# A four-layer graph kernel: the first attention stripe leaves out its last row group, which follows the start of the second stripe

## The chip, the cores and the metric

The kernel runs on one core of a Trainium2 chip. The metric is the device time of one execution in microseconds (us); the time before is the median of three runs. TensorE (PE) multiplies matrices into PSUM banks, ScalarE (ACT) applies functions and copies, VectorE (DVE) and GpSimd (POOL) work elementwise, SyncE (SP) issues most of the DMA transfers. Every engine takes its own instructions strictly in the order in which they were built, and waits at an instruction whose inputs are not there. What stands behind a waiting instruction on the same engine waits with it.

## The reference, cut to what matters

`x` has 4096 rows of 64 numbers, `adj` is a 4096 x 4096 matrix of zeros and ones. Four layers follow each other, each of the form `x = layernorm(x + layer(x, adj))`. Layers 1 and 3 are attention in hyperbolic space, and only they are touched by the change:

```
x_t   = logmap0(x)
left  = x_t @ w[:D];  right = x_t @ w[D:]
adj_att   = sigmoid(left[:, None] + right[None, :] + b) * adj
x_local   = logmap(x[:, None, :], x[None, :, :])
support_t = einsum('ij,ijd->id', adj_att, x_local)
out       = proj(expmap(x, support_t))
```

Layer 0 is a mean over neighbours with a matrix product and a normalisation, layer 2 a sum over neighbours with weights that halve from one neighbour to the next. Each layer reads the whole of `adj` again (268 MB in four passes).

## The kernel before, in words

**Tiles.** The output rows of a layer are cut into four *stripes* of 1024 (`GROUPS` = 3, 2, 1, 0, in this order), the source rows into 32 *blocks* of 128 (`BLOCKS`, from 31 down). Eight blocks are a *row group* with the same number as the stripe that holds the same rows. Two blocks are a *unit* `g` (15 down to 0): one transfer of 1 MB brings the edges of a unit (`load`, six buffers). A stripe of an attention layer thus has 16 units, four from each row group, and a layer 64 units. Units are counted here from 1 to 64 in the order of execution, in each attention layer.

**A unit** (`attend`, L1141 to L1216). For each of its two blocks: TensorE puts six matmuls into a PSUM tile `z` of 128 x 1024 (L1175, L1178, L1181; three `z` tiles exist); ScalarE makes `sig`, a sigmoid of `left` of the stripe and `right` of the block (L1136), and `sq`, a square of `z` (L1195); VectorE makes `t` = max(z, 0) * sig (L1198). Then VectorE combines the unit in one instruction of 128 x 2048 (L1203), and TensorE adds it, two units later, with float32 matmuls into `acc`, one PSUM bank (L1153; each counts as two passes in the profile). At the end of a stripe `acc` is copied by ScalarE to `sums` in SBUF (L1215). There is one `acc` bank, so the next stripe's first addition waits for that copy.

**Row work.** Whatever is done per row and not per pair is written as generators that give way at each `yield`; `tick` (after each block and unit, `rate` times) lets the queues of such generators go one step on, and the number that a generator yields is how many ticks it stays away. `later` puts a generator into one of three queues; a queue does its generators one after the other. `need(tag)` ticks until the named piece has been issued. The pieces:
- `end_0`, `norm_rows`, `prepare` (L1529 on, L929 on, L958 on): they end the layer before for one row group and make its inputs for the attention layer: `y`, the transposes `hi_lo`, `src`, `lo_hi`, `dst` (L1033 on TensorE, L1037 on ScalarE), `xe`, a logarithm (L1045, L1046 on ScalarE), `left` and `right`. For row group 0, the last one, most of this is on GpSimd ("pooled"): it is done while the first stripe of the attention layer already runs, since the first stripe needs row group 0 only in its last four units, 13 to 16.
- `far(small, large)` (L665) tells how many ticks such a chain on GpSimd takes: 0.29 us for a small and 1.04 us for a large operation, plus 3.9 us, divided by the length of a tick.
- `spread_left` (L1109): `left` of a stripe turned and copied to all partitions (L1117 on TensorE, two copies L1123 on ScalarE).
- `move(layer, s, sums, curve)`: after a stripe, its sums go through a centring product with the constant `centre` (L1286; L1265 for the very last stripe) to rows, and the map back to the next `x`. For stripes 3, 2, 1 the small operations are on GpSimd, with a few of them on VectorE (L1306, L1308, L783, L1353); for stripe 0 all are on VectorE.
- `supports` and `store`: what follows a moved stripe, for layer 2 or the output.

**Who orders.** In layers 0 and 2 the order on TensorE and ScalarE is that of the program. In the attention layers a scheduler in the compiler orders the instructions of every engine by its own estimate of when their inputs are there. From the second stripe on, `anchored` pins row work behind the pair work that was traced ahead of it; in the first stripe it may go where the scheduler likes.

`attention` (L1638) calls `attend` for stripes 3, 2, 1, 0. After each it queues the stripe's `move`. At the very end (L1825 on) a few VectorE operations fill `fits`, a test on the data; TensorE turns it (L1857), and only then does the last centring product (L1265) come on TensorE.

Of the kernel before, what the change touches and what calls it, by code (L numbers as in the profile page):

```python
# [19 lines left out]
P = 128  # L20
# [41 lines left out]
def gnn_stack_kernel(  # L62
# [504 lines left out]
    def stream(fits):  # L567

        with ExitStack() as st:
# [65 lines left out]
            def there(tag):  # L635
                while tag not in done:
                    yield 1
# [27 lines left out]
            def far(small, large=0):  # L665

                beat = {1: 0.8, 3: 0.4}.get(place[0], 1.6)
                return 1 + int((small * 0.29 + large * 1.04 + 3.9) / beat)

# [470 lines left out]

            def attend(layer, s, rate, then):  # L1141

                acc = ps.tile([P, W], F32, name="acc")
                if layer == 1 and s == GROUPS[0]:
                    spare.append(lambda dtype, shape: of_bank(acc, dtype, shape))
                lag, squares = [], []

                def add_up(g, t, ks, behind=None):

                    for k in ks:  # L1150
                        j = 2 * g + k
                        for h in range(2):
                            it = nc.tensor.matmul(  # L1153
                                acc[h * D : (h + 1) * D, :], xe[:, j, :],
                                t[:, k, h * W : (h + 1) * W],
                                start=j == BLOCKS[0], stop=j == BLOCKS[-1],
                            )
                            if behind is not None:
                                in_order(it.ins, behind.ins)

                for g in reversed(range(NB // 2)):
                    _, edge = load(s, g)
                    need((layer, 2 * g // WB))
                    if g == 4 and then is not None:
                        later(in_turn((layer, then, "left"), spread_left(then)), True)
                    for k in (1, 0):
# [17 lines left out]
                        if k == 1:  # L1184
                            if len(lag) == 2:
                                if spare:
                                    spare_ends()
                                add_up(*lag.pop(0), last)
                            sq = sb.tile([P, 2, WW], F32, name="sq")
                            t = sb.tile([P, 2, WW], F32, name="t", bufs=3)  # L1190
                            ts = [t, t]
                            if g == 0 and then is None and layer == 3:
                                ts[0] = sb.tile([P, 2, WW], F32, name="t", bufs=3)
# [18 lines left out]
                for args in lag:  # L1212
                    add_up(*args)
                sums = row.tile([P, W], F32, name="sums", bufs=2)
                nc.scalar.copy(sums, acc)  # L1215
                return sums  # L1216

            def to_rows_of(sums):

                t = take(F32, P, SB, 2, D)  # L1220
                for k in range(SB):
                    nc.tensor.transpose(t[:, k], sums[:, k * P : (k + 1) * P], ident)
                return t.rearrange("p k h f -> p h k f")

            def move(layer, s, sums, curve):
# [27 lines left out]
                if straight:  # L1253
# [5 lines left out]
                    for part in range(2):  # L1259
                        t = z_tile()[:, : 4 * (D + 1)].rearrange(  # L1260
                            "p (i h f) -> p i h f", i=2, h=2
                        )
                        for i in range(2):
                            cols = slice((2 * part + i) * P, (2 * part + i + 1) * P)
                            nc.tensor.matmul(  # L1265
                                t[:, i], sums[:, cols], centre, start=True, stop=True
                            )
                        parts.append(t)
# [12 lines left out]
                for part in () if straight else range(2):  # L1281
                    yield from free()
                    t = take(F32, P, 2, 2, D + 1)
                    for i in range(2):
                        cols = slice((2 * part + i) * P, (2 * part + i + 1) * P)
                        nc.tensor.matmul(t[:, i], sums[:, cols], centre, start=True, stop=True)  # L1286
                    yield near()
# [163 lines left out]
            with ExitStack() as lp:  # L1451
# [18 lines left out]

                x_ts = [row.tile([P, W], F32, name="sums", bufs=2)[: D + 1] for _ in range(2)]
                for x_t in x_ts:
# [89 lines left out]
                with tc.manual_schedule(engines=FIXED):  # L1562
                    for s in GROUPS:
# [44 lines left out]
                        if s == GROUPS[0]:  # L1608
                            need((0, s))
                            curve1, curve3, att1, att3 = made  # L1610
                        total = row.tile([P, W], F32, name="sums", bufs=2).rearrange(
                            "p (b d) -> p b d", d=D
# [25 lines left out]
            def attention(layer, curve, rates, behind):  # L1638

                need((layer, GROUPS[0]))  # L1640
                for n, s in enumerate(GROUPS):
                    if n:
                        need((layer, s, "turned"))
                        need((layer, s, "left"))
                    anchored[0] = n > 0
                    then = GROUPS[n + 1] if n + 1 < NW else None
                    if n == 0 and layer == 1:
                        later(end_0(GROUPS[-1], total, deg))
                    sums = attend(layer, s, rates[n], then)
                    move_s = in_turn((layer, s, "moved"), move(layer, s, sums, curve))  # L1650
                    if n:
                        later(
                            in_turn((layer + 1, s + 1), there((layer, s + 1, "moved")), behind(s + 1)),
                            True, 9,
                        )
                    apart = 2 if n + 1 == NW and layer == 1 else 0
                    later(move_s, apart)
                    if n + 1 == NW:
                        later(in_turn((layer + 1, s), behind(s)), apart)
                anchored[0] = False  # L1660
# [6 lines left out]
            )  # L1667
            attention(1, curve1, (2, 1, 1, 1), supports)

# [127 lines left out]
            with tc.manual_schedule(engines=FIXED):  # L1797
                spare.append(lambda dtype, shape: of_bank(row_bank, dtype, shape))

                for some in (GROUPS[:2], GROUPS[2:3], GROUPS[3:]):  # L1800
                    accs = wide_pass(some) if len(some) == 2 else narrow_pass(some[0])
                    for s, of in zip(some, accs):
                        sums = [row.tile([P, W], F32, name="sums", bufs=2) for _ in of]
                        for to, acc in zip(sums, of):
                            if s == GROUPS[-1]:
                                V.tensor_copy(to, acc)
                            else:
                                nc.scalar.copy(to, acc)
                        later(end_2(s, sums))
# [11 lines left out]
            with tc.issue_after(weighed[0].ins):  # L1821
                attention(3, curve3, (4, 1, 1, 1), store)

# [7 lines left out]

            sq = row.tile([P, D], F32, name="w_sq")
            V.memset(sq, 0.0)
            one = V.tensor_mul(sq[:D], w2_sb, w2_sb)
            in_order(one.ins, split[1].ins)
            ones = row.tile([P, 1], F32, name="w_ones")
            V.memset(ones, 1.0)
# [89 lines left out]
```

## Time and profile before

| | us |
|---|---|
| median of 3 runs (lowest, highest) | 1034.7 (1034.37, 1035.6) |
| the profiled execution's own time | 1035.3 |
| its span, first to last instruction | 1033.6 |
| PE / DVE / ACT / POOL busy | 940.1 / 910.2 / 747.0 / 333.9 |
| stretch of layer 0 | 0 to 171 |
| layer 1 (attention): its four stripes | 171, 260, 335, 412 to 488 |
| layer 2 | 488 to 692 |
| layer 3 (attention): its four stripes | 692, 779, 855, 931 to 1005 |
| last stripe's `move` and the output | 1005 to 1033.6 |

The execution has 1.7 us around its span, and is 0.6 us over the median of the runs. Mean granted TensorE clock 0.985. A row of the profile names line, engine, operation and tiles, then how often, busy us, mean ns of one, and the idle time of the engine just before it with what ended that idle time. In a timeline, a bracket at the end of a row is the engine's idle time before that row and the instruction that released it. "L1198 DVE" is line 1198 of the kernel, on VectorE; lines in the 760s and 780s are helpers that several callers share.

### The profile page before, as it was taken

The numbers are of one execution on the slowest core, as the hardware profiler recorded it, in microseconds if no ns is written. First come the engines' busy times: TensorE is split into PE (matmuls) and PEld (weight loads), VectorE is DVE, ScalarE is ACT, GpSimd is POOL, SyncE is SP. The second block draws the span as 40 slices with busy tenths as digits, with TensorE's granted clock in tenths as the row PEclk, the third lists the DMA queues.
The fourth block names the chain that finished last, engine by engine and source line by source line (L and its number), as shares of the span: only waits on it lengthen the run. The fifth ranks groups of instructions, "written<-read, shape, count | busy, mean of one in ns | idle before, by whom it ended". The sixth has DMA issues, their size and how long they took to land.

```text
span 1033.6 us, 14323 instructions
## 1 busy us (share of the span) xinstructions
PE 940.1 (91%) x5197; PEld 417.9 (40%) x5197; DVE 910.2 (88%) x1420; ACT 747.0 (72%) x866; POOL 333.9 (32%) x695
## 2 busy tenths in 40 slices
PE   7866767899999999999999999998999999999991
PEld 6755765233333333333333344442333333333320
DVE  7686797899999999999398499979999999999996
ACT  2102116789988988987677788888998898888860
POOL 0021211470255455365011020106302563662650
PEclk9999899999999999999999999999999999999996
DMA  9999999655666566575799998995465666665500
GB/s 369 425 427 425 397 426 425 260 189 204 235 216 230 200 224 224 179 244 204 268 351 351 373 335 311 337 325 198 164 244 201 213 240 216 239 209 208 205 10 14
DMA packets 38322, 271.68 MB, mean 263 GB/s; under 512 B 4255, under 2 KB 4577, under 8 KB 5474
## 3 DMA queue, kind: packets, MB, share of 16 engines
q1 hardware_dynamic: 37728, 270.03, 70.8%
q8 instruction: 42, 0.69, 0.3%
q10 hardware_dynamic: 514, 0.66, 0.2%
q14 instruction: 38, 0.31, 0.1%
HBM read 269.62 MB, written 1.05 MB: 262 GB/s over the span
## 4 chain that ended last, share of the span: by engine, by line
PE 60%; DVE 20%; DMA 7%; ACT 5%; POOL 5%; issue 2%; SPq 0%; ACTq 0%; POOLq 0%; DVEq 0%
PE acc L1153 17%; PE z L1774 11%; PE z L1175 8%; PE z L1181 7%; DVE t L1203 7%; PE z L1178 7%; DMA edges<-in_adj_dram 7%; DVE t L1198 6%; PE z L1786 3%; PE z L1740 2%; DVE junk L879 2%; ACT sq L1195 2%; PE acc L1584 2%; ACT sq L1781 1%; ACT sig L1136 1%
## 5 line engine op out<-in xcount | busy, mean ns | idle before, releaser
L1198 DVE SCALAR_TENSOR_TENSOR t<-z,sig 128x1024 f32<-128x1024 f32 x255 | 307.2, 1218 | 18.7 <-ACT sq L1195 16.5
L1195 ACT ACTIVATE sq<-z 128x1024 f32<-128x1024 f32 x256 | 255.2, 1023 | 60.0 <-PE z L1181 26.5
L1203 DVE SCALAR_TENSOR_TENSOR t<-sq,t 128x2048 f32<-128x2048 f32 x127 | 294.4, 2318 | 0.3
L1136 ACT ACTIVATE sig<-left_b,right 128x1024 f32<-128x1024 f32 x255 | 286.0, 1149 | 2.8 <-DVE t L1198 1.5
L1153 PE MATMUL acc<-t,xe 128*64 128x512 f32 x1024 | 256.6, 610 | 15.1 <-DVE t L1203 15.0
L1175 PE MATMUL z<-edges,two_i 128*128 128x512 bf16 x512 | 200.8, 392 | 2.5 <-DVE t L1198 1.5
L1181 PE MATMUL z<-dst,src 74*128 74x512 f16 x512 | 194.6, 380 | 0.0
L1178 PE MATMUL z<-lo_hi,hi_lo 128*128 128x512 f16 x512 | 193.6, 378 | 0.0
L1781 ACT ACTIVATE sq<-z 128x512 bf16<-128x512 f32 (+1 forms) x192 | 138.0, 740 | 39.8 <-PE z L1774 38.7
L1584 PE MATMUL acc<-parts,edges 128*128 128x193 bf16 x1024 | 100.2, 252 | 37.8 <-DMA edges<-in_adj_dram 37.0
L1153 PEld LDWEIGHTS acc<-t,xe 128*64 128x64 f32 x1024 | 64.0, 136 | 144.6 <-issue 105.6
L879 DVE SCALAR_TENSOR_TENSOR t<-edges 128x2048 bf16<-128x2048 f32 x41 | 94.0, 2308 | 20.0 <-DMA edges<-in_adj_dram 20.0
L1584 PEld LDWEIGHTS <-edges 128*128 128x128 bf16 x1024 | 86.7, 100 | 48.5 <-DMA edges<-in_adj_dram 46.4
L1175 PEld LDWEIGHTS <-two_i 128*128 128x128 bf16 x512 | 50.0, 98 | 121.7 <-issue 75.0
L1774 PE MATMUL z<-edges,pass_by 128*128 128x512 bf16 x248 | 86.5, 388 | 6.3 <-ACT sq L1781 5.7
L1774 PE MATMUL z<-edges,enter 128*128 128x512 bf16 x256 | 88.2, 387 | 0.0
L1181 PEld LDWEIGHTS <-src 74*128 74x128 f16 x512 | 49.1, 96 | 72.5 <-issue 10.3
L1178 PEld LDWEIGHTS <-hi_lo 128*128 128x128 f16 x512 | 50.2, 98 | 57.1 <-issue 11.5
L1303 POOL TENSOR_TENSOR w_att<-x,u 128x512 f32<-128x512 f32 x6 | 16.2, 2706 | 149.4 <-ACT u L1297 149.4
L979 ACT CAST ys<-y 128x512 f16<-128x512 f32 x8 | 4.9, 616 | 74.3 <-DVE y L976 44.6
L879 DVE SCALAR_TENSOR_TENSOR junk<-edges 128x2048 bf16<-128x2048 f32 x23 | 52.5, 2282 | 0.0
L1740 PE MATMUL z<-sq,halves 128*128 128x512 bf16 x128 | 48.0, 377 | 0.2 <-ACT sq L1781 0.2
(451 smaller groups left out, 906.4 us busy)
## 6 DMA issues: line engine op xcount, KB each, us to landing
edges<-in_adj_dram SPq DMA_DIRECT2D x256, 1024.0 KB, 5.0
x<-in_x_dram SPq DMA_DIRECT2D x2, 256.0 KB, 5.7
out_dram<-x ACTq DMA_DIRECT2D x2, 256.0 KB, 2.3
out_dram<-x SPq DMA_DIRECT2D x2, 256.0 KB, 2.8
x<-in_x_dram SPq DMA_DIRECT2D x1, 384.0 KB
x<-in_x_dram SPq DMA_DIRECT2D x1, 128.0 KB, 2.9
weights_sb<-in_weights_dram ACTq DMA_DIRECT2D x1, 96.0 KB, 5.5
enter_w<-in_enter_dram ACTq DMA_DIRECT2D x1, 32.5 KB
```

The source lines that it names most:

```text
L879: return V.scalar_tensor_tensor(junk, a, 0.0, a, ALU.not_equal, ALU.not_equal, accum_out=odd[:, n : n + 1])
L1136: one = nc.scalar.activation(sig, left_bs[s], AF.Sigmoid, bias=right[:, j : j + 1])
L1153: it = nc.tensor.matmul(acc[h * D : (h + 1) * D, :], xe[:, j, :], t[:, k, h * W : (h + 1) * W], start=j == BLOCKS[0], stop=j == BLOCKS[-1],)
L1175: nc.tensor.matmul(half, two_i, edge[:, at : at + W], start=True, stop=False)
L1178: nc.tensor.matmul(half, hi_lo[:, of], lo_hi[:, to], start=False, stop=False)
L1181: last = nc.tensor.matmul(half, src[:, of], dst[:, to], start=False, stop=True)
L1195: square = nc.scalar.activation(sq[:, k], zp, AF.Square, bias=ROOT + OFF, scale=-1.0 / UNIT)
L1198: V.scalar_tensor_tensor(ts[k][:, k], zp, 0.0, sig, ALU.max, ALU.mult)
L1203: V.scalar_tensor_tensor(t, sq, HIGH**2, t, ALU.add, ALU.mult)
L1584: nc.tensor.matmul(banks[i // 2][:, i % 2, :PARTS], edge[:, at : at + P], parts[:, j, :PARTS], start=j == BLOCKS[0] and i % 2 == 0, stop=j ...
L1774: nc.tensor.matmul(z[:, h : h + W], lhs, rhs[:, h : h + W], start=j == BLOCKS[0], stop=True, skip_group_check=True,)
L1781: weighed[0] = nc.scalar.activation(w, z[:, :n], AF.Exp, bias=-(OFF_EDGE + CUT) * LN2, scale=-LN2)
```

## The change

In each attention layer six *sections* take the place of four stripes:

| section | stripe | row groups | units in the order |
|---|---|---|---|
| 1 | 3 | 3, 2, 1 | 1 to 12 |
| 2 | 2 | 3 | 13 to 16 |
| 3 | 3 | 0 | 17 to 20 |
| 4 | 2 | 2, 1, 0 | 21 to 32 |
| 5 | 1 | all | 33 to 48 |
| 6 | 0 | all | 49 to 64 |

Sections 1 and 2 end with a copy of `acc` to a `sums` tile and nothing else. After sections 3 to 6 the stripe's `move` is queued; for stripes 3 and 2 it gets two `sums` tiles and adds them in the centring product, which becomes twice as many matmuls (`to_centre`). Row work is pinned from section 4 on. Stripe 2's `left` is spread from the third queue, five units ahead of the end of section 1. `far` counts 6.0 us instead of 3.9. A third `sums` buffer is added, and two small tiles of the last test are laid into a constant that is no longer used then.

```
-                return 1 + int((small * 0.29 + large * 1.04 + 3.9) / beat)
+                return 1 + int((small * 0.29 + large * 1.04 + 6.0) / beat)
...
-            def attend(layer, s, rate, then):
+            def attend(layer, s, rate, then, groups, final):
 
+                gs = [g for g in reversed(range(NB // 2)) if 2 * g // WB in groups]
+                j_first, j_last = 2 * gs[0] + 1, 2 * gs[-1]
                 acc = ps.tile([P, W], F32, name="acc")
...
-                                start=j == BLOCKS[0], stop=j == BLOCKS[-1],
+                                start=j == j_first, stop=j == j_last,
...
-                for g in reversed(range(NB // 2)):
+                for g in gs:
                     _, edge = load(s, g)
                     need((layer, 2 * g // WB))
-                    if g == 4 and then is not None:
-                        later(in_turn((layer, then, "left"), spread_left(then)), True)
+                    if g == gs[max(len(gs) - 5, 0)] and then is not None:
+                        later(
+                            in_turn((layer, then, "left"), spread_left(then)),
+                            2 if s == GROUPS[0] else 1,
+                        )
...
-                sums = row.tile([P, W], F32, name="sums", bufs=2)
+                sums = row.tile([P, W], F32, name="sums", bufs=3)
                 nc.scalar.copy(sums, acc)
                 return sums
...
+            def to_centre(to, sums, cols):
+
+                for n, part in enumerate(sums):
+                    nc.tensor.matmul(
+                        to, part[:, cols], centre, start=n == 0, stop=n + 1 == len(sums)
+                    )
...
-                        nc.tensor.matmul(t[:, i], sums[:, cols], centre, start=True, stop=True)
+                        to_centre(t[:, i], sums, cols)
...
-                for n, s in enumerate(GROUPS):
-                    if n:
+                g3, g2, g1, g0 = GROUPS
+                sections = (
+                    (g3, g2, (g3, g2, g1), False),
+                    (g2, None, (g3,), False),
+                    (g3, None, (g0,), True),
+                    (g2, g1, (g2, g1, g0), True),
+                    (g1, g0, GROUPS, True),
+                    (g0, None, GROUPS, True),
+                )
+                sums, before = {s: [] for s in GROUPS}, None
+                for n, (s, then, groups, final) in enumerate(sections):
+                    if n in (1, 4, 5):
                         need((layer, s, "turned"))
                         need((layer, s, "left"))
-                    anchored[0] = n > 0
-                    then = GROUPS[n + 1] if n + 1 < NW else None
+                    anchored[0] = n > 2
...
-                    sums = attend(layer, s, rates[n], then)
-                    move_s = in_turn((layer, s, "moved"), move(layer, s, sums, curve))
-                    if n:
+                    sums[s].append(attend(layer, s, rates[n], then, groups, final))
+                    if not final:
+                        continue
+                    move_s = in_turn((layer, s, "moved"), move(layer, s, sums[s], curve))
+                    if before is not None:
                         later(
...
-            attention(1, curve1, (2, 1, 1, 1), supports)
+            attention(1, curve1, (2, 2, 2, 1, 1, 1), supports)
...
-                attention(3, curve3, (4, 1, 1, 1), store)
+                attention(3, curve3, (4, 4, 4, 1, 1, 1), store)
...
-            sq = row.tile([P, D], F32, name="w_sq")
-            V.memset(sq, 0.0)
-            one = V.tensor_mul(sq[:D], w2_sb, w2_sb)
-            in_order(one.ins, split[1].ins)
-            ones = row.tile([P, 1], F32, name="w_ones")
+            sq, ones = enter_w[:D, :D], enter_w[:D, D : D + 1]
+            V.tensor_mul(sq, w2_sb, w2_sb)
             V.memset(ones, 1.0)
```

## The prediction

> **What bounds the kernel now.** I read the page first (VectorE 88% busy, TensorE 91%), then busy time by stretch, then VectorE's, ScalarE's and GpSimd's timelines in the first stripes, then the tail. First the stretches (each row: TensorE, its weight loads, VectorE, ScalarE, GpSimd busy, then clock and DMA share):
>
> ```profile
> 171.00:260.00 89.00, 81.18 (x378) 29.56 (x379) 80.24 (x88) 76.33 (x81) 34.15 (x56) 0.98 0.64 238
> 260.00:335.00 75.00, 75.00 (x334) 26.72 (x333) 74.04 (x55) 67.22 (x72) 35.18 (x88) 1.00 0.65 228
> 692.00:779.00 87.00, 80.68 (x392) 30.69 (x391) 81.12 (x87) 78.91 (x85) 24.61 (x43) 1.00 0.61 214
> 779.00:855.00 76.00, 76.00 (x333) 26.88 (x332) 73.69 (x54) 66.79 (x71) 37.34 (x88) 1.00 0.63 218
> ```
>
> Both attention layers behave alike. A later stripe takes 75 to 76 us with VectorE and TensorE full: the undisturbed unit is 4.57 us from one L1203 to the next (one combine, 2.20, and two L1198 at about 1.15). A first stripe takes 87 to 89. Of those 12 to 14 us, the row work of group 0 on VectorE is 8.7 in layer 1 and 7.4 in layer 3 (sum of its rows), which the change does not remove. The rest is VectorE idle: 7.1 in layer 1 from unit 2 on, 3.9 in layer 3. Who ends the idle time in layer 1:
>
> ```profile
> 189.44 0.69 DVE L932 TENSOR_REDUCE n_m<-z 128x8 f32<-128x512 f32 x1 [2.87 <-POOL z L1545]
> 210.72 0.20 DVE L970 RECIPROCAL rb<-b 128x8 f32<-128x8 f32 x1 [1.09 <-POOL b L967]
> 230.66 1.23 DVE L1198 SCALAR_TENSOR_TENSOR t<-z,sig 128x1024 f32<-128x1024 f32 x1 [0.72 <-ACT sq L1195]
> ```
>
> Two waits on GpSimd's chain, then small waits on ScalarE. The second kind has its cause on ScalarE's own timeline:
>
> ```profile
> 214.77 0.62 ACT L979 CAST ys<-y 128x512 f16<-128x512 f32 x1 [3.21 <-POOL y L976]
> 228.00 1.28 ACT L1045 ACT_TABLE_LOAD   x1
> 229.50 0.21 ACT L1045 ACTIVATE tt<-tt 128x8 f32<-128x8 f32 x1 [0.22 <-POOL tt L1015]
> 230.74 1.28 ACT L1136 ACT_TABLE_LOAD   x1
> 232.03 1.15 ACT L1136 ACTIVATE sig<-left_b,right 128x1024 f32<-128x1024 f32 x1
> ```
>
> ScalarE loses 3.21 on GpSimd, then has four copies L1037, the logarithms and two table loads to make up, beside 3.9 a unit of pair work. The logarithm met its input almost exactly (0.22). GpSimd's small operations take 0.20, but every eighth to tenth takes over 2:
>
> ```profile
> 226.51 2.35 POOL L798 TENSOR_TENSOR rt<-rs_t,rt 128x8 f32<-128x8 f32 x1
> 228.94 0.20 POOL L1014 TENSOR_TENSOR tt<-q,rt 128x8 f32<-128x8 f32 x1
> ```
>
> **The change part by part.** The idea has room for at most the idle time, 7.1 + 3.9 = 11 us. What of it goes is read from the built order of instructions of the changed kernel, with the durations above.
>
> *First stripe, layer 1.* Up to L932 VectorE's order is the same, so 2.87 stays. The second pair, L783 to L970, moves one unit later as a whole, with the same work between: 1.09 stays. Then the chain to the logarithm. Before, VectorE's L783 for it stands behind the 17th L1198, and L1045 behind ScalarE's 21st square: four blocks apart. After, L783 stands behind the 21st L1198 and L1045 behind the 22nd square: one apart, so that GpSimd has three blocks less, some 6 us. By hand: L984 at 224.3; GpSimd from L989 to the end of L1015 took 216.57 to 229.47, 12.9, with three long operations (12.9 - 3 x 2.15 = 6.4 without any); so its input comes between 230.8 and 237.3. ScalarE is there at 230.6. I take 2.3 long ones, 236: a wait of about 5. Behind it on ScalarE stand two squares, a table load and the next sigmoid (0.9 + 0.9 + 1.3 + 1.05); VectorE has two L1198 and a combine left, then stands until 240. Also the two logarithms are now apart with sigmoids between: four table loads for two, 2 x 1.29 = 2.6 more on ScalarE, which has 0.67 a unit to spare. Followed instruction by instruction, the 16th combine comes at 264 against 258.8 before. About 0.7 of that is made up where the copies L1123 went into ScalarE's idle 3.9 at 188. **+4.5 us, from 0 (no long operation) to +6.5.**
>
> [...]
>
> *First stripe, layer 3.* L783 to L970 has a combine less between (idle 1.37 becomes 3.6, +2.3). In exchange copies and row work, which before crowd into units 6 to 9 (1.87 idle in the ninth), spread over three more units. By hand the 12th combine (before at 757.9) comes at the same place within 0.1. **0, from -1.9 to +2.3.**
>
> *Two more section ends per layer, four in all.* Each drains two units into `acc` and copies it (0.59 on ScalarE, which has room). The unit after the first stripe's end lost 0.47 before. **4 x 0.3 = +1.2, from 0 to 2.0.**
>
> *Twice the centring matmuls for stripes 3 and 2.* Eight more passes a stripe. Four of them put the next matmul off by 0.45 (265.26 to 265.71) and 0.62, so 1.07 a stripe, 4.3 in all, on an engine with under 0.1 a unit to spare; VectorE's 1.34 of reductions beside it covers half. **+2.2, from 0 to 4.3.**
>
> *Stripes 2 and 1 move later.* Stripe 3's move starts four units later, and its queue is serial, so the moves of 2 and 1 start three to four units behind their stripe's end. Before, copies L1297 and L1304 met the section end and VectorE idled 0.99, 0.91, 0.99, 0.92 there (sum 3.8); apart from it I take half. **-1.9, from -3.8 to 0.**
>
> *The tail.* Stripe 1's move now isn't done when the last unit ends. Before:
>
> ```profile
> 1002.49 2.64 DVE L1203 SCALAR_TENSOR_TENSOR t<-sq,t 128x2048 f32<-128x2048 f32 x1
> 1005.05 1.21 DVE L1198 SCALAR_TENSOR_TENSOR t<-z,sig 128x1024 f32<-128x1024 f32 x1
> 1008.82 0.16 DVE L1843 TENSOR_TENSOR fits<-fits,g 128x1 f32<-128x1 f32 x1
> ...
> 1010.47 0.27 PE L1857 MATMUL fit_t<-ident,fits 128*1 128x128 f32 x1
> 1011.22 1.16 PE L1265 MATMUL z<-centre,sums 128*128 128x130 f32 x8 [0.48 <-ACT sums L1215]
> ```
>
> After, the chain's L783 for `mt` stands behind that combine (1005.05), the next L783 (for `w`) stands ahead of L1843, and between the two GpSimd does its small operations, as here:
>
> ```profile
> 986.36 0.17 DVE L783 TENSOR_SCALAR n<-mt 128x8 int32<-128x8 int32 x1
> ...
> 993.29 0.20 POOL L1380 TENSOR_SCALAR w<-w 128x8 f32<-128x8 f32 x1
> ```
>
> That is 7.1 with one long operation. So VectorE stands until 1012.2, `fits` is done at 1012.9, L1857 at 1013.0, and L1265, behind it on TensorE, at 1013.2 instead of 1011.22. The whole last move hangs on L1265. **+2.0, from 0 (no long operation, 1010.2) to +4.** Stripe 1's output then goes out about 1023 to 1026, ahead of the last one at 1028.3: nothing. Of SP's edge loads none is added and DMA is at 0.61 to 0.65 there: nothing. At the start of layer 2 the same pair of L783 holds VectorE some 3.5 us; layer 2 has TensorE busy 197.4 of 204 and VectorE only 157.2, which covers it: 0, up to +1 if the held edge checks delay a load.
>
> Sum: 4.5 + 0 + 1.2 + 2.2 - 1.9 + 2.0 = **+8.0**. Against the profiled execution: span 1033.6 + 8.0 = 1041.6, time 1035.3 + 8.0 = 1043.3; that execution lies 0.6 over the median, so 1034.7 + 8.0 = **1042.7 us**. All low ends give -5.7, all high ends +20.1.
>
> **Rivals.**
> 1. *It pays* (the other side). GpSimd's chain was on the path for the first 60 us of layer 1, and group 0 now has four more units. If at most one long operation falls between L989 and L1015, the input is there by 233 and ScalarE's 2.4 of VectorE waits in units 10 to 13 dissolve (-2.4); layer 3 at its low end (-1.9), ends +0.6, centring +1.0, later moves -1.9, tail 0: -4.6, 1030. It decides with the logarithm's input at 233 or sooner. For it: the relaxed deadline is real. Against: about one long operation in nine, and some 21 operations in that chain.
> 2. *A tie.* The two chains come out even (0 for layer 1 and the tail): 1.2 + 2.2 - 1.9 = +1.5, 1036.2.
> 3. *The joints dominate.* Each new end costs what units 18 to 20 lost in layer 3 beyond their row work (16.3 - 3 x 4.57 - 1.36 = 1.2), as PE has nothing to run ahead on: 4.8, centring 4.3, the rest as forecast: 4.5 + 4.8 + 4.3 - 1.9 + 2.0 = +13.7, 1048.4. For it: TensorE and VectorE are both near full. Against: the first end in layer 1 lost 0.47.
>
> **How the numbers follow.** Forecast (new waits on GpSimd in layer 1 and the tail) 0.52, own range 1038 to 1046.5; rival 1 0.17; rival 2 0.17; rival 3 0.14. The 8-in-10 range leaves out rival 1 and takes in the rest: 1033 to 1050. 0.2% is 2.1 us, about what a measurement of this kernel can tell from no change. Faster is rival 1, 0.17. Rival 2 lies at +1.5, mostly within: same 0.15. Slower 0.68.
>
> **What would show it.** In the changed profile: an idle of some 5 us on ScalarE ahead of L1045 in layer 1, released by POOL `tt`, and VectorE idle behind it; four table loads there instead of two; 2.87 ahead of L932 unchanged; in the tail a wait of over 3 us on VectorE ahead of an L783, released by POOL, with L1265 starting some 8 us behind the end of the last combine of 128 x 2048 (6.2 before). It is wrong if ScalarE never waits for `tt`, or if VectorE's idle time in the first 20 units of both layers falls below 11.

## The result: 12.2 us slower

After the change the median is **1046.88 us** (1045.74 to 1047.95, 5 runs) against 1034.7 (1034.37 to 1036.41, 5 runs) before: ratio 1.0113, interval 1.0098 to 1.0128. The profiled execution of the changed kernel took 1047.95, with a span of 1046.2 (1033.6 before): 12.6 us to be found. The changed kernel's lines from 1144 on stand a few lines further down: L1153 is L1155 now, L1198 is L1203, L1203 is L1208, L1195 is L1200, L1265 and L1286 have become one line of `to_centre`, L1233, L1843 is L1864 and L1857 is L1878.

The stretches again, with the two of layer 3 taken 10 us later than before, as that layer starts later (columns as before):

```profile
171.00:260.00 89.00, 74.94 (x344) 27.54 (x346) 71.89 (x85) 71.09 (x77) 31.92 (x56) 0.96 0.61 226
260.00:335.00 75.00, 74.90 (x333) 27.16 (x330) 72.38 (x52) 67.38 (x72) 21.44 (x54) 1.00 0.61 210
702.00:789.00 87.00, 81.33 (x389) 31.09 (x390) 78.87 (x87) 78.03 (x85) 24.90 (x43) 0.98 0.59 208
789.00:865.00 76.00, 76.00 (x338) 27.44 (x337) 72.70 (x53) 66.57 (x71) 27.29 (x73) 1.00 0.63 214
```

In the first 89 us of layer 1 VectorE is busy 71.9 for 80.2 before. The other stretches differ by 1.0 to 2.3. To place the loss I cut each span at VectorE's 128 x 2048 combines, which every kernel has in the same order: **A** and **D** are the first 16 units of layer 1 and layer 3 (start of the 1st combine to start of the 16th), **B** and **E** the rest of that layer, **C** the way from layer 1 to layer 3, **F** from the start of the last wide combine to the end of the span. (What is left is ahead of A: 176.0 to 178.1 everywhere.) The table has every kernel of this study; stages are of one profiled execution each, the time is the median, the ratio is to the kernel before on the same chip.

| kernel | A | B | C | D | E | F | time | ratio (interval) |
|---|---|---|---|---|---|---|---|---|
| before | 82.0 | 229.9 | 209.5 | 78.2 | 226.1 | 31.1 | 1034.7 | |
| changed | 89.9 | 231.1 | 209.1 | 79.4 | 225.4 | 34.2 | 1046.9 | 1.0113 (1.0098, 1.0128) |
| e1, layer 1 only | 88.2 | 231.1 | 209.2 | 78.3 | 226.1 | 31.1 | 1042.4 | 1.0075 (1.0062, 1.0088) |
| e2, layer 3 only | 81.3 | 229.9 | 209.5 | 80.1 | 225.4 | 34.1 | 1039.2 | 1.0044 (1.0031, 1.0057) |
| e3, far 3.9 | 80.6 | 231.1 | 209.5 | 78.1 | 225.7 | 34.1 | 1037.9 | 1.0032 (1.0021, 1.0044) |
| e4, logarithms held | 82.9 | 231.1 | 209.5 | 79.1 | 225.7 | 34.2 | 1040.7 | 1.0063 (1.0048, 1.0078) |
| e5, pinned | 81.2 | 231.1 | 209.6 | 76.1 | 225.7 | 34.1 | 1036.5 | 1.0013 (1.0004, 1.0022) |
| e6, fits first | 88.7 | 231.1 | 209.2 | 79.2 | 225.4 | 33.1 | 1045.3 | 1.0105 (1.0089, 1.0120) |
| e7, no wide GpSimd tail | 88.8 | 231.1 | 209.2 | 79.2 | 225.0 | 32.9 | 1044.2 | 1.0087 (1.0073, 1.0101) |
| e8, one centring | 89.6 | 229.0 | 209.4 | 79.1 | 224.2 | 34.0 | 1043.1 | 1.0081 (1.0067, 1.0095) |
| e9, before with far 6.0 | 89.1 | 230.7 | 209.2 | 84.0 | 225.7 | 30.2 | 1047.3 | 1.0117 (1.0100, 1.0133) |
| e10, before pinned | 84.4 | 229.9 | 209.6 | 81.1 | 226.0 | 30.3 | 1039.6 | 1.0043 (1.0029, 1.0056) |
| e11, mended | 81.2 | 231.5 | 212.3 | 75.1 | 225.4 | 33.1 | 1037.6 | 1.0025 (1.0016, 1.0033) |
| e12, layer 3, mended | 83.2 | 230.0 | 209.7 | 75.1 | 226.2 | 31.3 | 1033.9 | 0.9989 (0.9980, 0.9998) |

Changed minus before: A +8.0, B +1.2, C -0.4, D +1.1, E -0.7, F +3.1, and 0.3 ahead of A. Two places carry it: the first stripe of layer 1 and the tail.

**The first stripe of layer 1.** ScalarE's timeline of the changed kernel (start, duration, idle before and its releaser):

```profile
221.34 0.62 ACT L979 CAST ys<-y 128x512 f16<-128x512 f32 x1 [3.21 <-POOL y L976]
231.85 1.28 ACT L1045 ACT_TABLE_LOAD   x1
237.81 0.21 ACT L1045 ACTIVATE tt<-tt 128x8 f32<-128x8 f32 x1 [4.68 <-POOL tt L1015]
239.86 1.28 ACT L1136 ACT_TABLE_LOAD   x1
246.98 1.28 ACT L1046 ACT_TABLE_LOAD   x1
248.50 1.28 ACT L1136 ACT_TABLE_LOAD   x1
```

The logarithm L1045, which had waited 0.22, waits 4.68 for GpSimd, and there are four table loads. VectorE behind it, and at the two other places that changed:

```profile
189.72 0.69 DVE L932 TENSOR_REDUCE n_m<-z 128x8 f32<-128x512 f32 x1 [2.87 <-POOL z L1555]
199.92 1.23 DVE L1203 SCALAR_TENSOR_TENSOR t<-z,sig 128x1024 f32<-128x1024 f32 x1 [1.64 <-ACT sq L1200]
201.87 1.23 DVE L1203 SCALAR_TENSOR_TENSOR t<-z,sig 128x1024 f32<-128x1024 f32 x1 [0.72 <-ACT sq L1200]
217.29 0.20 DVE L970 RECIPROCAL rb<-b 128x8 f32<-128x8 f32 x1 [1.09 <-POOL b L967]
223.43 1.23 DVE L1203 SCALAR_TENSOR_TENSOR t<-z,sig 128x1024 f32<-128x1024 f32 x1 [1.52 <-ACT sq L1200]
...
238.96 2.36 DVE L1203 SCALAR_TENSOR_TENSOR t<-z,sig 128x1024 f32<-128x1024 f32 x2 [2.98 <-ACT sq L1200]
243.25 1.23 DVE L1203 SCALAR_TENSOR_TENSOR t<-z,sig 128x1024 f32<-128x1024 f32 x1 [1.93 <-ACT sq L1200]
```

Idle in the first 16 units: 15.5, for 7.1 before. 2.87 and 1.09 are as they were; 2.98 and 1.93 are the logarithm's wait, 1.52 that of L979; 1.64 and 0.72 ahead of them come behind 6.8 us at half speed (below), where before has 0.60 behind 3.4.

**The tail**, VectorE:

```profile
1011.98 2.28 DVE L1208 SCALAR_TENSOR_TENSOR t<-sq,t 128x2048 f32<-128x2048 f32 x1
1014.18 0.17 DVE L783 TENSOR_SCALAR n<-mt 128x8 int32<-128x8 int32 x1
...
1021.08 0.17 DVE L783 TENSOR_SCALAR n<-w 128x8 int32<-128x8 int32 x1 [3.28 <-POOL w L1390]
...
1021.34 0.20 DVE L1864 TENSOR_TENSOR fits<-fits,g 128x1 f32<-128x1 f32 x1
...
1024.94 0.63 DVE L764 SCALAR_TENSOR_TENSOR k<-d,k_c,ys 128x8 f32<-128x8 f32 x1
1025.61 0.96 DVE L1323 TENSOR_TENSOR k<-k,rb 128x8 f32<-128x8 f32 x1
...
1026.80 1.03 DVE L764 SCALAR_TENSOR_TENSOR t<-d,kx 128x8 f32<-128x8 f32 x1
```

L783 waits 3.28 for GpSimd ahead of `fits`; the last centring product L1233 starts at 1021.71, 9.73 after the start of the last wide combine (8.73 before): +1.0. The other 2.05 are the last three rows. Before, the same three took 0.23, 0.17 and 0.17:

```profile
1014.56 0.23 DVE L764 SCALAR_TENSOR_TENSOR k<-d,k_c,ys 128x8 f32<-128x8 f32 x1
1014.82 0.17 DVE L1313 TENSOR_TENSOR k<-k,rb 128x8 f32<-128x8 f32 x1
...
1015.23 0.17 DVE L764 SCALAR_TENSOR_TENSOR t<-d,kx 128x8 f32<-128x8 f32 x1
```

Beside the long ones GpSimd runs the last wide operations of stripe 1's move:

```profile
1024.50 1.04 POOL L1395 TENSOR_TENSOR w_att<-x,p 128x512 f32<-128x512 f32 x1
1025.50 1.04 POOL L1400 TENSOR_TENSOR u<-u,q 128x512 f32<-128x512 f32 x1
1026.62 1.18 POOL L1403 TENSOR_TENSOR x<-u,w_att 128x512 f32<-128x512 f32 x1
```

### The profile page after: what moved, and what is told of

It reads as the page before. It is cut to its first block, busy times and chain, and to the rows that moved or that the text cites. A ratio compares the mean times of both kernels' runs of the same rounds, so it can differ in the third digit from the quotient of the medians.

```text
span 1046.2 us, 14390 instructions
## 1 busy us (share of the span) xinstructions
PE 941.8 (90%) x5229; PEld 421.0 (40%) x5229; DVE 909.3 (87%) x1419; ACT 751.0 (72%) x872; POOL 320.6 (31%) x695
## 4 chain that ended last, share of the span: by engine, by line
PE 64%; DVE 17%; DMA 7%; ACT 6%; POOL 4%; issue 2%; ACTq 0%; POOLq 0%; SPq 0%; DVEq 0%
PE acc L1155 18%; PE z L1798 11%; PE z L1180 9%; PE z L1186 8%; PE z L1183 8%; DMA edges<-in_adj_dram 6%; DVE t L1208 4%; DVE t L1203 4%; PE z L1810 3%; DVE junk L879 2%; PE z L1764 2%; ACT sq L1200 2%; PE acc L1594 1%; ACT sq L1805 1%; PE aux L1233 1%
## 5 line engine op out<-in xcount | busy, mean ns | idle before, releaser
L1203 DVE SCALAR_TENSOR_TENSOR t<-z,sig 128x1024 f32<-128x1024 f32 x255 | 308.1, 1219 | 29.6 <-ACT sq L1200 27.5
L1200 ACT ACTIVATE sq<-z 128x1024 f32<-128x1024 f32 x256 | 254.8, 1022 | 57.0 <-PE z L1186 26.6
L1208 DVE SCALAR_TENSOR_TENSOR t<-sq,t 128x2048 f32<-128x2048 f32 x127 | 292.0, 2299 | 0.4
L1155 PE MATMUL acc<-t,xe 128*64 128x512 f32 x1024 | 257.1, 616 | 16.1 <-DVE t L1208 15.6
L1594 PE MATMUL acc<-parts,edges 128*128 128x193 bf16 x1024 | 97.9, 249 | 39.9 <-DMA edges<-in_adj_dram 39.0
L1155 PEld LDWEIGHTS acc<-t,xe 128*64 128x64 f32 x1024 | 64.0, 138 | 144.8 <-issue 102.9
L1186 PEld LDWEIGHTS <-src 74*128 74x128 f16 x512 | 49.3, 96 | 75.1 <-issue 11.9
L979 ACT CAST ys<-y 128x512 f16<-128x512 f32 x8 | 4.9, 616 | 76.5 <-DVE y L976 45.6
L1313 POOL TENSOR_TENSOR w_att<-x,u 128x512 f32<-128x512 f32 x6 | 10.4, 1727 | 152.7 <-ACT u L1307 152.7
```

Of the source, the lines that this page charges most:

```text
L1155: it = nc.tensor.matmul(acc[h * D : (h + 1) * D, :], xe[:, j, :], t[:, k, h * W : (h + 1) * W], start=j == j_first, stop=j == j_last,)
L1186: last = nc.tensor.matmul(half, src[:, of], dst[:, to], start=False, stop=True)
L1200: square = nc.scalar.activation(sq[:, k], zp, AF.Square, bias=ROOT + OFF, scale=-1.0 / UNIT)
L1203: V.scalar_tensor_tensor(ts[k][:, k], zp, 0.0, sig, ALU.max, ALU.mult)
L1208: V.scalar_tensor_tensor(t, sq, HIGH**2, t, ALU.add, ALU.mult)
L1594: nc.tensor.matmul(banks[i // 2][:, i % 2, :PARTS], edge[:, at : at + P], parts[:, j, :PARTS], start=j == BLOCKS[0] and i % 2 == 0, stop=j ...
```

## The experiments

Theory *waits*: the loss is the new waits on GpSimd (first stripe of layer 1, tail). Rival *joints*: each section end and each doubled centring product costs, in both layers alike.

### e1 and e2: the sections in one layer

Each keeps the new sections, and `far` at 6.0, in layer 1 (e1) or layer 3 (e2) alone; the other layer has its four stripes and 3.9 (e1 shown; e2 has 3 for 1):

```
+                apart_too = layer == 1
+                if not apart_too:
+                    sections = tuple(
+                        (s, (*GROUPS[1:], None)[n], GROUPS, True) for n, s in enumerate(GROUPS)
+                    )
+                    rates = (rates[0], *rates[3:])
...
-                return 1 + int((small * 0.29 + large * 1.04 + 6.0) / beat)
+                return 1 + int((small * 0.29 + large * 1.04 + (6.0 if place[0] == 1 else 3.9)) / beat)
```

> Sections in layer 1 alone (with 6.0 in far there), layer 3 as before the change (four stripes, 3.9). Theory 'waits' (the loss is made by row work that stands too early in an engine's queue and waits for GpSimd, most of it in layer 1's first stripe): 8.0 of layer 1's first 16 units and 1.2 of the rest of layer 1, tail as before: +9, about 1043.7. Rival 'joints' (each section end and each doubled centring product costs, wherever it is): half of the sections, half of the 12 lost: +6, about 1040.7.

> Sections in layer 3 alone (with 6.0 in far there), layer 1 as before the change. 'Waits': first 16 units of layer 3 +1.1, the rest of it -0.7, the tail +3.1, so +3.5, about 1038.2, with over 3 us of VectorE idle ahead of an L783 in the tail. 'Joints': half of the 12 lost, +6, about 1040.7.

1042.4 and 1039.2. Against the kernel before on the same chip the losses are 7.6 and 4.4, 11.9 of the 12.2 together. By time alone both lie between the two theories; the stretches decide. e1 has A at 88.2 and the tail of before; e2 has the tail of the changed kernel and A of before (its D is 1.9 over before, where 1.1 was expected). *Joints* would have shown in B and E, which are +1.2 and -0.7. It falls as the main cause.

### e3: the old count in `far`

```
-                return 1 + int((small * 0.29 + large * 1.04 + 6.0) / beat)
+                return 1 + int((small * 0.29 + large * 1.04 + 3.9) / beat)
```

> All sections, but far counts 3.9 us again. 'Waits': in the built order the row work of group 0 in layer 1's first stripe then stands where it stood before the change, the logarithms side by side with two table loads, so about 7 of the 8.0 of layer 1's first 16 units go, the tail stays: about 1040, no ScalarE idle over 1 us ahead of L1045. 'Joints': the sections are the same, so 1046.9 within 1.

1037.9, at 1.0032: A falls from 89.9 to 80.6, and D from 79.4 to 78.1; the tail stays at 34.1. L1045 waits 0.23 there. So nine of the twelve microseconds hang on the count in `far`, with the sections in place.

### e4: both logarithms behind the second copy

```
+                            in_order(one.ins, copies[1].ins)
+                            in_order(two.ins, copies[1].ins)
```

> As the changed kernel, but for row group 0 both logarithms (L1045, L1046) are pinned on ScalarE behind the second of the four copies L1037; in the built order they then stand side by side, three squares later, with two table loads instead of four in layer 1. 'Waits': the 4.68 of ScalarE idle ahead of the logarithm and 2.6 of table loads go, 4 to 6 of the 8.0 come back: 1041 to 1043. 'Joints': nothing to gain, 1046.9 within 1.

1040.7; A is 82.9, with two table loads. Pinning two instructions of 0.2 us on ScalarE behind a copy gives 7 of the 8 us of A back, and 6.2 of the time. (The scheduler then also puts L1055 of VectorE two blocks later.) GpSimd's chain, from L783 on VectorE to the end of L1014, takes 7.4 us in both kernels: the place of the wait is what cost, not the length of the chain.

### e9: the count in `far` alone, in the kernel before

```
-                return 1 + int((small * 0.29 + large * 1.04 + 3.9) / beat)
+                return 1 + int((small * 0.29 + large * 1.04 + 6.0) / beat)
```

> The kernel before with far counting 6.0 us in place of 3.9 and nothing else changed. If the loss needs both, the later due times and the room that the new sections give the scheduler (theory), the need at unit 13 pulls the chain of group 0 along as before and the first stripe of layer 1 stays within 2 us of its 82.0: 1034 to 1037. If the longer count alone carries the loss (rival), that stretch grows by 5 to 8: 1040 to 1043.

1047.3, ratio 1.0117: as slow as the whole change, **without a single section**. My theory for this run (both are needed) fell, and the rival's 1040 to 1043 was too low, since the stretch of layer 3 grew too. ScalarE's timeline of e9:

```profile
217.22 0.62 ACT L979 CAST ys<-y 128x512 f16<-128x512 f32 x1 [3.20 <-POOL y L976]
227.74 1.28 ACT L1045 ACT_TABLE_LOAD   x1
233.69 0.21 ACT L1045 ACTIVATE tt<-tt 128x8 f32<-128x8 f32 x1 [4.67 <-POOL tt L1015]
```

The wait is 4.67 here and 4.68 in the changed kernel. In both, L783 stands behind the 21st of the 128 x 1024 operations on VectorE and L1045 behind the 22nd square on ScalarE; with 3.9 (before and e3) they stand behind the 17th and the 21st. So the later count, not the sections, moved L783 four pair blocks back and L1045 one. The rest of the first stripe is not the same in both. In e9 VectorE's L932 stands one block later and waits 1.17 in place of 2.87, and there are two table loads, not four; but all of ScalarE's next sigmoids stand behind three of the copies L1037, and VectorE waits for them:

```profile
191.37 0.69 DVE L932 TENSOR_REDUCE n_m<-z 128x8 f32<-128x512 f32 x1 [1.17 <-POOL z L1545]
247.79 1.22 DVE L1198 SCALAR_TENSOR_TENSOR t<-z,sig 128x1024 f32<-128x1024 f32 x1 [4.56 <-ACT sig L1136]
```

So A is 7.1 over before in e9 and 8.0 in the changed kernel, by the same wait at L1045 but in part by other ones. In layer 3, e9 has the same wait (4.00 ahead of L1045) and D at 84.0; there the sections of the changed kernel give 4.6 of that back (79.4), which is the gain that they do bring. In layer 1 they bring none that A shows (89.9 and 89.1).

### e5 and e10: row work pinned

e5 is the changed kernel, e10 the kernel before, with row work pinned behind the pair work from the start:

```
-                    anchored[0] = n > 2
+                    anchored[0] = True
```

> The changed kernel with row work pinned behind the pair work traced ahead of it in every section, the first three too. In its built order the two logarithms stand side by side again, with two table loads in place of four. If the waits come from where the scheduler put ScalarE's and VectorE's instructions of the chain of group 0 (theory), the stretch of the first 16 units of layer 1, 89.9 us, falls to 83 to 86 and the time to 1041 to 1044; the tail stays at 34.1. If the length of GpSimd's chain itself is what delays group 0 (rival), the wait moves to another instruction and the stretch stays at 89 or more: 1046 to 1048.

> The kernel before with row work pinned in the first stripe too. With the sections, pinning gave 81.2 in the first 16 units of layer 1 and 76.1 in those of layer 3 (82.0 and 78.2 before). If the sections bring the 2.1 of layer 3 (theory: group 0's work has four more units to spread over), this kernel shows 78 or more there and 1034 to 1037. If pinning alone brings it (rival), layer 3 falls to 76 and, without the new tail and the doubled centring, the time to 1031 to 1033.

e5: 1036.5, ratio 1.0013, 10.4 less than the changed kernel and better than the 1041 to 1044 expected, as D falls too. A is 81.2 and D 76.1, 2.1 under the kernel before. ScalarE's timeline of e5:

```profile
220.99 0.62 ACT L979 CAST ys<-y 128x512 f16<-128x512 f32 x1 [0.42 <-POOL y L976]
240.05 1.28 ACT L1045 ACT_TABLE_LOAD   x1
241.34 0.21 ACT L1045 ACTIVATE tt<-tt 128x8 f32<-128x8 f32 x1
241.46 0.19 ACT L1046 ACTIVATE q<-q 128x8 f32<-128x8 f32 x1
```

Neither wait is left: L1045 stands where its input has been there for 4 us, and the logarithms share a load. The rival (the wait moves elsewhere) fell. e10 shows that pinning is no gain in itself: without the sections it costs 2.4 in A and 2.8 in D (1039.6, 1.0043; 1034 to 1037 was expected). Only with both, room and order, does the first stripe of layer 3 fall below before. (e5 counts 6.0 and e10 3.9, so the count is not held apart in this pair.)

### e6 and e7: the tail

e6 puts stripe 1's L783 for `w` behind the last operation on `fits`:

```
+                    if behind_fits:
+                        in_order(one.ins, behind_fits[0].ins)
...
-            V.tensor_mul(fits, fits, g)
+            behind_fits.append(V.tensor_mul(fits, fits, g))
```

e7 leaves out the three wide GpSimd operations of stripe 1, with a ScalarE copy in their place, so that stripe 1's output is not the result:

```
+                if layer == 3 and s == 1:
+                    nc.scalar.copy(x_of(4)[:, at, :], u)
+                    yield pool_done(15, 3)
+                    return
```

> The changed kernel with the last stripe-1 chain's integer operation L783 put behind the last operation on fits, so that fits no longer waits for GpSimd. If the order of these two is worth what the tail showed (the last centring product starts 9.73 us after the start of the last wide combine, 8.73 before), the tail falls from 34.2 by 1.0 and the time to 1045.9. Rival: GpSimd's three wide operations then meet the last move's small ones at another place and take the gain back: 1046.9, no change.

> The changed kernel, in which the last three 512-wide GpSimd operations of stripe 1 in layer 3 are left out and one ScalarE copy takes their place, so that the output rows of stripe 1 are not the map's result. If VectorE's small operations of the last move are long (0.63, 0.96, 1.03 us for 0.23, 0.17, 0.17 before) because GpSimd runs wide operations beside them (theory), they fall back to about 0.2 and the time falls by 1.5 to 2.1: 1044.8 to 1045.4. If they are long for another reason, such as where the tail starts (rival), the time stays at 1046.9.

e6: F is 33.1, down 1.07, and the time 1045.3, as expected (A is 1.2 lower as well, with 3.4 us at half speed for 6.8, see below). But L783 still waits 2.90 for GpSimd, now behind `fits`, and GpSimd's wide operations now meet three other instructions of VectorE (0.93, 0.97 and 1.02 for 0.17). e7: F is 32.9, and the same rows of VectorE are short again:

```profile
1023.54 0.23 DVE L764 SCALAR_TENSOR_TENSOR k<-d,k_c,ys 128x8 f32<-128x8 f32 x1
1023.81 0.17 DVE L1323 TENSOR_TENSOR k<-k,rb 128x8 f32<-128x8 f32 x1
...
1024.21 0.17 DVE L764 SCALAR_TENSOR_TENSOR t<-d,kx 128x8 f32<-128x8 f32 x1
```

So the second part of the tail's loss is VectorE held up beside wide GpSimd operations. F fell by 1.3 and not 2.05, since the rows ahead of these came later: L1316 starts 12.49 behind the start of the last wide combine, 11.57 in the changed kernel. The clock gives 0.88 of that: in e7 the granted clock is 0.50 from 1018.7 on, and the last centring product takes 1.94, where the changed kernel, at 1.00 there, takes 1.06:

```profile
1019.42 1.94 PE L1233 MATMUL z<-centre,sums 128*128 128x130 f32 x8
1020.00:1022.00 2.00, 1.36 (x7) 1.06 (x5) 0.72 (x3) 0.82 (x3) 1.42 (x8) 0.50 0.00 0
```

### e8: one centring product

```
-                for n, part in enumerate(sums):
...
+                part = sums[-1]
+                nc.tensor.matmul(to, part[:, cols], centre, start=True, stop=True)
```

> The changed kernel, in which only the last sums tile of a stripe goes through the centring product; the first part of the sums of stripes 3 and 2 is left out of the result. That takes away the doubled centring alone. The prediction gave it 2.2 us (0 to 4.3): 1044.7. If TensorE makes the extra passes up in waits that are there anyway (rival), 1046.4 to 1047, and the rest of layer 1, 231.1, stays 1.2 over its 229.9 before.

e8 leaves the first part of the sums out of the result. 1043.1 (1044.7 was expected). B falls by 2.1 and E by 1.2, 3.3 in all: that is what the doubled centring costs. B and E together are only 0.5 over before in the changed kernel; that the later moves hide the rest is inferred and was not tested.

### e11 and e12: a kernel under both?

e11 has the changes of e5 and e6, and in layer 1 one GpSimd addition in place of the doubled centring:

```
+                if len(sums) == 2 and layer == 1:
+                    nc.gpsimd.tensor_add(sums[1], sums[1], sums[0])
+                    sums = sums[1:]
+                    yield G.wait(0, 1)
```

> The changed kernel with row work pinned in every section, the operation L783 of the tail behind fits, and in layer 1 the two sums tiles added by one GpSimd operation of 128 x 512 at the start of the move in place of doubled centring. If the gains add (theory): 1036.5 with pinning, less 1.1 in the tail, less 2.1 in the rest of layer 1: 1033.3, at or just under the kernel before. If the GpSimd addition holds VectorE up beside it as in the tail (rival), the rest of layer 1 stays near 231: 1035.4.

1037.6, over both forecasts (1033.3 and 1035.4): B stays at 231.5, and C grows by 2.7 over e5. The waits of TensorE in B name the reason for the one, VectorE's timeline at the start of layer 2 that for the other:

```profile
PE aux L1235 <- POOL sums L1268: 1.5, 1, 1.5
```

```profile
494.85 0.17 DVE L783 TENSOR_SCALAR n<-mt 128x8 int32<-128x8 int32 x1 [2.48 <-POOL mt L1383]
500.05 0.17 DVE L783 TENSOR_SCALAR n<-w 128x8 int32<-128x8 int32 x1 [5.03 <-POOL w L1396]
```

TensorE waits 1.5 for the addition (L1235 is `to_centre` there; what else B did not gain was not followed up). The three turns more in each of two moves make stripe 1's move later: L783 for `w` is at 500.05, in e5 at 496.38, and VectorE stands 7.5 ahead of the two rows, 3.7 in e5. e12 has sections in layer 3 alone, pinned, with `fits` first, and shortens the serial queue of moves:

```
+                if layer == 3 and s in GROUPS[:2]:
+                    yield 4
+                    return
                 yield pool_done(15, 3) if G.on_pool else after(72)
```

> Sections in layer 3 alone, with row work pinned in all of them and far at 6.0 there, at 3.9 elsewhere. In layer 3 the last wait of the moves of stripes 3 and 2 is cut from 9 turns to 4, so that the next move starts five turns sooner, and the store of those stripes waits the five turns instead; in the built order L783 for w stands a unit ahead of the last wide combine again. If the long tail comes from stripe 1's move starting too late (theory), the stretch from the last wide combine on is 31.1 again, and with the first stripe of layer 3 at 76 and its rest at 225.7 the time is 1032 to 1033, under the kernel before. If cutting the wait only makes the next move's first instructions stand behind GpSimd (rival), the rest of layer 3 grows by 1 to 3 and the time is 1034 to 1036.

1033.9, ratio 0.9989 (0.9980 to 0.9998): 1.3 us under the kernel before, and 0.9 over the 1032 to 1033 of the theory. D is 75.1 (3.1 under before), as in e11; F is 31.3, where e11 has 33.1. L783 for `w` now stands 2.4 us ahead of the last wide combine, so the tail's length came from the start of stripe 1's move. E is at 226.2, not 225.7, so 0.5 of what the rival expected is there. A, where its order is that of before, is at 83.2, with 6.8 us at half speed for 3.4 (below).

## Why the prediction was right, step by step

The sign and both waits were right, and so were the signs named for them: 4.68 on ScalarE ahead of L1045, four table loads, 2.87 ahead of L932, 3.28 ahead of an L783 in the tail, and 22 us of VectorE idle in the first 20 units of both layers (13 before); L1233 starts 7.5 behind the end of the last wide combine, where 8 was named. The size was not: +8.0 forecast, +12.2 measured. 1046.9 lies in the range of 1033 to 1050, but just over the 1038 to 1046.5 that the forecast gave itself; that it lies inside is in part luck, by the width that rival 3 lent the range. Three terms of the sum were too small, and one of its mechanisms was told wrongly.

- *First stripe, layer 1, +4.5 (0 to +6.5).* Measured +8.0, over the upper end. Part of that is the clock: the granted clock was 0.50 about L932's wait for 6.8 us in the changed kernel (191.7 to 198.5) and for 3.4 before (193.5 to 196.9). With equal clock the stripe costs 6.4 to 6.9 more: A is 89.9 and 89.6 (changed, e8) against 83.2 (e12) with 6.8 us of it, and 88.7 and 88.8 (e6, e7) against 82.0 (before) with 3.4. The wait itself was right: 11.7 us from L984 to GpSimd's end forecast, 10.8 measured (226.99 to 237.78); wait 5 and 4.68; VectorE on again at 240 and 238.96; four loads; 2.87 and 1.09 unchanged. What was missed is 1.52 that VectorE now loses to the wait of L979, which was there before at the same 3.21 but cost VectorE nothing. The 0.7 that L1123 was to give back shows in e3 against e2, both without the half speed: 80.6, with the copies early, and 81.3.
- *The idle time to be won.* Row work of 8.7 and idle time of 7.1 are 15.8, more than the 14 that they were to explain. From the stages: A of 82.0 less 15 units of 4.57 is 13.4, of which 7.1 is idle, so the row work costs 6.3.
- *Whose fault it was.* The prediction read the order of the changed kernel and booked its cost to the change as a whole; e9 shows that one constant of it does this alone.
- *Long operations.* "Every eighth to tenth takes over 2" was read as chance, and rival 1 was priced by it. It is not chance: 53 of the 61 long ones of before end with a combine of VectorE (below). Between L989 and L1015 of the changed kernel two operations are long (2.17 and 2.26) and VectorE runs two combines; before, it was three and three.
- *First stripe, layer 3, 0 (-1.9 to +2.3).* +1.1: held.
- *Section ends +1.2, centring +2.2, later moves -1.9.* Together +1.5; B and E together +0.5. The centring was mis-sized: 3.3 by e8, so the other two are -2.8 together. They were not parted further. (Of the four new section ends two lie in A and D.)
- *Layer 2, 0.* -0.4: held. e11 shows the price when that cover goes: +2.7.
- *The tail, +2.0.* +3.1. The step that failed is "Stripe 1's output then goes out ... ahead of the last one: nothing". As a transfer it cost nothing; the three operations that make it cost 2.05 on VectorE. The order of L783 and `fits` cost 1.0, half of the forecast: the combine ahead of it took 2.28 for 2.64, the chain 6.9 for 7.1, and the way from L783 to L1233 0.6 for 1.0. The clock has a part here too. Before and in the changed kernel TensorE runs 3.4 us of the tail at half speed (the last sixteen matmuls into `acc` take 5.35 and 5.31 there, where eight take 1.94 at clock 1.00), which puts off the last sums and so hides some of the wait: before, L1265 waits 0.48 for them. In e9 and e10, with the order of before but without the half speed, the last centring product starts 7.86 behind the last wide combine and F is 30.2 and 30.3; in e3 and e8, with the order of the changed kernel and also without it, it starts at 9.70 and 9.73 and F is 34.1 and 34.0. At full clock the order thus costs 1.9, and the tail 3.8.
- *Rivals.* 3, at 1048.4, was nearest in time, but by a cause that e1, e2 and e8 refute: the section ends, centring and later moves of both layers came to 0.5, not to the 7.2 that it put on them. 1 and 2 stand or fall with the first stripe: with the old count (e3) or pinned (e5) the times are 1037.9 and 1036.5, about rival 2's 1036.2, though not by its terms: the tail stays 3.0 longer in both.

## What to carry to other kernels

A constant that tells a scheduler when an input will be there is part of a change like any other: try it alone before the rest is judged, since here it was worth as much as the whole (1.0117 and 1.0113). When a producer's instruction is moved back by four blocks and its consumer on another engine by one, count the difference in the built orders; that found the wait to within half a microsecond. Room given to one stage is taken from a serial queue's last entry: look at what ends last in the tail before handing it out. And compare a stretch only between executions with the same granted clock in it: here that moved A by up to 1.9 us and the tail by 0.9.

## What the runs showed of the hardware

**Long operations of GpSimd and VectorE lie beside each other.** VectorE's and GpSimd's timelines of the changed kernel, side by side:

```profile
230.16 2.28 DVE L1208 SCALAR_TENSOR_TENSOR t<-sq,t 128x2048 f32<-128x2048 f32 x1
...
233.71 2.28 DVE L1208 SCALAR_TENSOR_TENSOR t<-sq,t 128x2048 f32<-128x2048 f32 x1
```

```profile
230.33 2.17 POOL L787 TENSOR_TENSOR rs_t<-rt 128x8 f32<-128x8 f32 x1
...
233.78 2.26 POOL L794 TENSOR_TENSOR rt<-rs_t,rt 128x8 f32<-128x8 f32 x1
```

Both long GpSimd operations start inside a combine of VectorE and end with it (232.50 and 232.44, 236.04 and 235.99). In the trace of before, 61 of GpSimd's 128 x 8 operations took over 0.6 us; 53 of them lie beside L1203 and end 0.09 us (median) behind it. Of the 546 shorter ones, 509 have their middle inside an L1198, which reads `z` from PSUM, and 3 inside an L1203. No run moved a combine to test this; the matching ends are the evidence. In the tail it goes the other way: VectorE's operations of 0.23, 0.17 and 0.17 take 0.63, 0.96 and 1.03 beside GpSimd's wide ones of 1.04 to 1.18, and 0.23, 0.17 and 0.17 again in e7 without them. Beside the pair operation with `z` in PSUM those 509 of GpSimd's took 0.20 (median).

**TensorE at half speed about the wait at L932.** While VectorE waits at L932, TensorE idles 3.44. The stretches behind it (columns as above; the last three are granted clock, DMA share, GB/s):

```profile
192.00:194.00 2.00, 1.34 (x4) 0.54 (x6) 2.00 (x4) 1.25 (x2) 0.04 (x1) 0.50 0.01 4
194.00:196.00 2.00, 2.00 (x6) 0.24 (x2) 2.00 (x3) 1.94 (x2) 1.92 (x2) 0.50 0.00 0
196.00:198.00 2.00, 2.00 (x7) 0.62 (x6) 2.00 (x2) 0.13 (x1) 0.12 (x1) 0.50 0.00 0
198.00:200.00 2.00, 2.00 (x10) 0.85 (x9) 0.36 (x2) 1.14 (x2) 0.00 (x0) 0.88 0.49 86
```

Eight matmuls L1155 take 3.68 there, 2.59 in the same place before (L1153), and 1.94 in e1, which idles the same 3.44 and keeps clock 1.00:

```profile
188.00:200.00 12.00, 8.56 (x38) 2.84 (x37) 11.16 (x10) 8.37 (x9) 2.88 (x3) 1.00 0.58 213
```

So kernels that are alike up to here lose between 0 and 2 us at this place, by execution. Among kernels of one order that is most of the spread of A: 81.3 without the half speed (e2), 82.0 with 3.4 us of it (before), 83.2 with 6.8 (e12). In the changed kernel the granted clock falls to 0.50 at 191.7, 727.6 and 1014.3 and rises again at 198.5, 731.0 and 1017.7, so after 6.83, 3.41 and 3.41 us; before, the four such stretches that end within the span take 3.41 each. In both traces all of these times lie whole multiples of 3.413 us apart (within 0.1): 727.6 - 191.7 is 157 times it, 1014.3 - 727.6 is 84 times it. They keep no fixed distance from TensorE's idle: in the changed kernel it lasts from 189.2 to 192.7 and the clock falls at 191.7; before, from 188.9 to 192.4, and the clock falls at 193.5. Why e1 escaped, no run here shows.
